# Keys of a cross-attention from quarter products: two of seven half products per whole chunk made in seven smaller ones

## The chip, the core and the metric

The kernel runs on one core of one Trainium2 chip. The metric is the time of the whole program on the device in microseconds. The engines named here are TensorE (PE, with its weight loads PEld), VectorE (DVE), ScalarE (ACT), GpSimd (POOL) and SyncE (SP), which issues the DMAs.

## The reference

One block of a perceiver: 128 latent rows attend to 12,544 context rows, then attend to themselves, then pass a mixture of experts. All is float32. What matters here is the first part, the cross-attention to the context (`cond`, 12,544 x 512), with 8 key and value groups of 128 columns and 16 query heads:

```python
def _L0_xattn_ref(...):
    ...
    kvx = jnp.einsum('bsi,oi->bso', cond, w_kv_x)
    kx, vx = jnp.split(kvx, 2, axis=-1)
    kx = _ln(kx.reshape(b, sc, g, d), kxln_w, kxln_b)
    vx = vx.reshape(b, sc, g, d)
    xout = _gqa(qx, kx, vx).reshape(b, s, nh * d)
    cat = jnp.concatenate([core, xout], axis=-1)
    catq = _div_clamp_fp8(cat, proj_smooth)
    return jnp.einsum('bsi,oi->bso', catq, wproj) * (proj_in_scale * proj_w_scale)
```

So keys and values are each the product of a 12,544 x 512 matrix with a 512 x 1024 one, the keys are normalised per group over their 128 columns, and a softmax attention runs over all 12,544 rows.

## The kernel before

**Chunks.** The context is cut into 25 chunks of 512 rows; number 12 has 256. Chunk 0 is worked in part beside the preparation of the queries. A chunk is `whole(c)` when it is not the first and has 512 rows: 23 of the 25. The loop over `c` has two stages. In the scores stage, eight groups `g` are gone through: `scores(c, g)` (PE L824) multiplies keys and queries, ACT scales them (L829), DVE takes maxima (L835); between the groups one piece each of the value products of this chunk is issued. In the key stage, eight pieces of the key products of chunk `c + 1` are issued by `keys`, and after each piece `others(g)` runs `maxima` and `outputs(c, g)` (PE L930), which weighs the values of chunk `c`.

**Products with seven in place of eight.** Weights and tokens are cut into halves in both directions, and a product of two 2 x 2 block matrices is made from seven block products (Winograd's form of Strassen's scheme). `mixed[c]` holds the seven token factors, `mixed_w` the seven weight factors; sums and differences of the tokens are made by `mix_tokens` on POOL. Two of the four quarters of the original are still used as they stand; the difference `b22 - b12` is written over `b12`, `a11 - a21` over `a21`. `unit` (L330) runs the seven products of one unit in three PSUM banks: bank `a` is copied out by ACT three times (`held`, L339) while products go on being accumulated on it, and DVE adds the other banks to the copies (L345, L353, L358). `k_unit` makes the keys so, in two units of four groups; each of the seven products is four matmuls of 256 columns (L369). `v_unit` makes the values so in chunks that are not whole.

**Values one level deeper.** For whole chunks, `v_chunk` makes two of the seven half products (numbers 1 and 3) from seven products of quarters each time, `fine(...)` (L449). The quarters' token differences come from `mix_finer_tokens` on POOL (L425 to L428), into a tile `fx` of one buffer; those of the weights come once, in chunk 0, from `mix_finer_weights` on POOL (L408 to L411).

**Banks and temporaries.** Key and value products share a pool of three PSUM banks, `ps_kv`, tag "kv": a new tile waits until an old one has been read for the last time. ACT's copies go to SBUF tiles of tag "u", three of them. In `v_chunk` the last bank `a` is read by two DVE adds (L501, L502), the last bank `d` by one (L499).

**Softmax.** `maxima(c, 4)` and `maxima(c, 8)` call `max_rows`: small DVE reductions (L852, L862) and arithmetic (L867 to L875). Then, for each pair `j` of groups, `spread` puts the shifts on all partitions (L884), DVE subtracts them (L900), and `weigh` takes exponentials on ACT (L912), and rescales and sums rows on POOL (L914, L922). Pairs 0 and 1 are handled in the scores stage, 2 and 3 in the key stage.

**Norm of the keys.** `k_sums` squares the finished keys on ACT (L511) and sums on DVE (L512), four heads at a time; `k_rstd` folds them by small matmuls on PE (L524), and POOL takes the power (L531).

**Order.** The order of the instructions on each engine is laid down when the program is built: written order gives the priority, and an instruction that is expected to be ready can go ahead of one that is not. `tc.issue_after(x)` holds the instructions in its block behind `x` on their engine. At run time each engine works through its list in that order.

Of the kernel before, what the change touches and what calls it, by code (L numbers as in the profile page):

```python
# [9 lines left out]
F32 = mybir.dt.float32  # L10
# [7 lines left out]
P = 128  # L18
# [27 lines left out]
def block_kernel(  # L46
# [56 lines left out]
    make_identity(nc, ident)  # L103
    mhalf = keep.tile([P, 16], F32, name="mhalf")
    nc.gpsimd.memset(mhalf, -0.5)
    ones = keep.tile([P, P], F32, name="ones")
    nc.gpsimd.memset(ones, 1.0)
    fold = keep.tile([P, 32], F32, name="fold")
    rcol = keep.tile([P, NCOL], F32, name="rcol")
# [219 lines left out]
    def unit(mm, view, d11, d12, d21, d22):  # L329


        a = ps_kv.tile([P, CH], F32, tag="kv", name="a_ps")
        b = ps_kv.tile([P, CH], F32, tag="kv", name="b_ps2")
        c = ps_kv.tile([P, CH], F32, tag="kv", name="c_ps")
        va, vb, vc = view(a), view(b), view(c)

        def held(name):
            t = tmpk.tile([P, CH], F32, tag="u", name=name, bufs=3)
            copied[0] = nc.scalar.copy(view(t), va).ins  # L339
            return view(t)  # L340

        mm(a, 0, True)
        p1 = held("p1")
        mm(b, 1, True)
        nc.vector.tensor_tensor(d11, vb, p1, ALU.add)  # L345
        yield
        mm(a, 5, False)
        u2 = held("u2")
        mm(c, 4, True)
        yield  # L350
        mm(a, 6, False)
        u3 = held("u3")
        nc.vector.tensor_tensor(d22, vc, u3, ALU.add)  # L353
        yield
        mm(a, 3, False)
        nc.scalar.copy(d21, va)
        mm(c, 2, False)
        added[0] = nc.vector.tensor_tensor(d12, vc, u2, ALU.add).ins  # L358
        yield
# [38 lines left out]

    finer = []

    def finer_w(i, k):

        return wkv[:, 2 + k, :, H + i * H // 2 : H + (i + 1) * H // 2]

    def mix_finer_weights(eng):
        finer.append(finp.tile([P, 4, 2, H // 2], F32, name="finer"))
        s1, s2, s3, s4 = (finer[0][:, i] for i in range(4))
        eng.tensor_tensor(s1, finer_w(1, 0), finer_w(1, 1), ALU.add)  # L408
        eng.tensor_tensor(s2, s1, finer_w(0, 0), ALU.subtract)
        eng.tensor_tensor(s3, finer_w(0, 0), finer_w(1, 0), ALU.subtract)  # L410
        eng.tensor_tensor(s4, finer_w(0, 1), s2, ALU.subtract)  # L411

    finer_x = {}

# [1 line left out]
        return c > 0 and chunks[c][1] == CH  # L416

    def mix_finer_tokens(c, eng):
        t = finp.tile([P, 2, 4, P], F32, tag="fx", name=f"finer_{c}")
        finer_x[c] = []  # L420
        for i, x in enumerate((mixed[c][1], mixed[c][3])):
            b11, b12 = x[:, 0, 0:P], x[:, 0, P : 2 * P]
            b21, b22 = x[:, 1, 0:P], x[:, 1, P : 2 * P]
            t1, t2, t3, t4 = (t[:, i, j, :] for j in range(4))
            eng.tensor_tensor(t1, b12, b11, ALU.subtract)  # L425
            eng.tensor_tensor(t2, b22, t1, ALU.subtract)
            eng.tensor_tensor(t3, b22, b12, ALU.subtract)
            eng.tensor_tensor(t4, b21, t2, ALU.subtract)  # L428
            finer_x[c].append((b11, b21, b22, t4, t1, t2, t3))

    def v_chunk(c):

        f = (
            finer_w(0, 0), finer_w(0, 1), finer[0][:, 3], finer_w(1, 1), finer[0][:, 0],
            finer[0][:, 1], finer[0][:, 2],
        )
        xs = finer_x.pop(c)

        def bank(name):
            return ps_kv.tile([P, CH], F32, tag="kv", name=name)  # L440

        def held(a, name):
            t = tmpk.tile([P, CH], F32, tag="u", name=name, bufs=3)
            copied[0] = nc.scalar.copy(t, a).ins
            return t

        def fine(ps, n, first):
            for i in range(2):
                nc.tensor.matmul(  # L449
                    ps[:, i * H // 2 : (i + 1) * H // 2], lhsT=xs[i][n], rhs=f[n][:, i, :],  # L450
                    start=first and i == 0, stop=True, skip_group_check=True,
                )

        def both(t):
            return t.rearrange("p (i o) -> p i o", i=2)

        def to(o, v):
            return V[:, v, :].rearrange("p (i c o) -> p i c o", i=2, c=2)[:, :, o, :]

        a, b = bank("fa_ps"), bank("fb_ps")  # L460
        fine(a, 0, True)
        p1 = held(a, "p1")
        fine(b, 1, True)
        nc.vector.tensor_tensor(to(0, 0), both(b), both(p1), ALU.add)
        yield
        fine(a, 5, False)
        u2 = held(a, "u2")
        d = bank("fc_ps")
        fine(d, 4, True)
        yield  # L470
        fine(a, 6, False)
        u3 = held(a, "u3")
        nc.vector.tensor_tensor(to(1, 1), both(d), both(u3), ALU.add)
        yield
        fine(a, 3, False)
        nc.scalar.copy(to(1, 0), both(a))
        fine(d, 2, False)
        nc.vector.tensor_tensor(to(0, 1), both(d), both(u2), ALU.add)
        yield
        for v in range(2):  # L480
            def mm(ps, i, first):
                w, x = mixed_w[i], mixed[c][i]
                for k in range(2):
                    last_mm[0] = nc.tensor.matmul(  # L484
                        ps, lhsT=x[:, k, v * P : (v + 1) * P], rhs=w[:, k, H : 2 * H],
                        start=first and k == 0, stop=k == 1, skip_group_check=True,
                    ).ins

            t1, t2 = V[:, v, :], V[:, 2 + v, :]
            a, d = bank("a_ps"), bank("c_ps")  # L490
            mm(a, 0, True)
            nc.vector.tensor_tensor(t1[:, :H], a, t1[:, :H], ALU.add)
            mm(d, 4, True)
            nc.scalar.copy(t2[:, H:], d)
            yield
            mm(a, 5, False)
            u2 = held(a, "u2")
            mm(d, 2, False)
            nc.vector.tensor_tensor(t2[:, :H], d, u2, ALU.add)  # L499
            mm(a, 6, False)  # L500
            nc.vector.tensor_tensor(t2[:, H:], a, t2[:, H:], ALU.add)  # L501
            added[0] = nc.vector.tensor_tensor(t1[:, H:], a, t1[:, H:], ALU.add).ins  # L502
            yield
# [38 lines left out]
    def keys(c, others, pool, tag, todo=None, done=0):  # L542

        sums = {}
        todo = todo or parts(k_unit(c, u) for u in range(2))
        for i in range(done, 8):
            next(todo)
            if i % 4 == 3:
                sums[i // 4] = k_sums(c, i // 4)
            if others:  # L550
                others(i)
            if i == (6 if others else 4):
                with ExitStack() as first:
                    if not others:
                        first.enter_context(tc.high_priority())
                        first.enter_context(tc.issue_after(cores[2]))
                    k_rstd(c, 0, sums.pop(0), pool, tag)
        return sums

    with tc.tile_pool(name="pre", bufs=2) as pre, tc.tile_pool(name="pre1", bufs=1) as pre1, tc.tile_pool(  # L560
# [115 lines left out]
            begin(names[0])  # L676
        with tc.issue_after(begun[0][1]):
            nc.tensor.transpose(psb[:, :P], gains[:, 3:4].to_broadcast([P, P]), ident)
            nc.tensor.matmul(psb[:, P:], lhsT=ones, rhs=gains[:, 5:6], start=True, stop=True)
            nc.scalar.copy(kb, psb)  # L680
        for k in range(NK):
            wk_in = wkvT[k * P : (k + 1) * P, : G * D].rearrange("p (u h o) -> p u h o", u=2, h=2)
# [117 lines left out]


    finp = main.enter_context(tc.tile_pool(name="finp", bufs=1))
    olp = late.enter_context(tc.tile_pool(name="olp", bufs=1, side="right", reuse_waits="tile"))
    ol = [olp.tile([P, 2, HS], F32, name=f"ol{g}") for g in range(G)]
    rlat = keep.tile([S, NH], F32, name="rlat")
# [168 lines left out]
    def maxima(c, i):  # L974

        if i in (4, 8):
            max_rows(c, i // 2 - 2, 2)
        j = i // 4 * 2 - 2 + (i - 1) % 4
        if i in (5, 6, 9, 10):

            last = copied[0]
            if c == 0 and i == 6:
                weigh(c, 0, last)
            if c == NCH // 2 and i == 10:
                weigh(c, 2, last)
            spread(c, j)
            if (c, j) in ((0, 0), (NCH // 2, 2)):
                return
            wait = (c, j) in ((0, 3), (NCH // 2 - 1, 2)) or whole(c) and j == 0
            weigh(c, j, last if wait else None)  # L990

    for c in range(NCH):
# [7 lines left out]
        for g in range(G):  # L1000
# [10 lines left out]
            if g == 2 and c + 1 < NCH:  # L1011
                with tc.issue_after(summed[0] if c else made):
                    for step in mix_tokens(c + 1):
                        step()
                    if c == 0:
                        mix_finer_weights(nc.gpsimd)
            if g == 4 and c + 1 < NCH and whole(c + 1):
                mix_finer_tokens(c + 1, nc.gpsimd)

# [1 line left out]
        def others(g):  # L1021
            maxima(c, G + g)
            outputs(c, g)

        if c + 1 < NCH:
            sums = keys(c + 1, others, ps_t, "t")
# [386 lines left out]
```

## Time and profile before

| | |
|---|---|
| median of 3 runs | 2154.01 us (2148.28, 2154.01, 2210.41) |
| profiled execution | 2148.35 us, of which the span from first to last instruction 2146.6 us |
| granted TensorE clock | 1.000 |
| busy: PE, DVE, ACT, POOL | 2121.8, 1366.1, 918.5, 1174.8 us |
| before the chunk loop | 126.7 us |
| chunks 0, 11 and 12 | 61.8, 65.5 and 53.2 us |
| each other chunk up to 23 | 75.8 us: scores stage 37.4, key stage 38.4 |
| from the scores of chunk 24 on | 247.8 us |

The chunk that the prediction reads closely is number 5: its scores stage begins at 491.69 us from the span's start, its key stage (keys of chunk 6) at 529.10, and the next chunk's scores at 567.47. In a row of the profile, "x8" counts instructions, and an fp32 matmul as written in the kernel is two of them. The ends of matmuls are modelled and overlap, so distances are taken from start to start.

### The profile page before, as it was taken

How to read it: one execution, taken by the hardware profiler on the slowest of the kernel's cores; microseconds unless marked ns; L12 is line 12 of the kernel's file. 1: busy time of each engine (PE TensorE's matmuls, PEld its weight loads, DVE VectorE, ACT ScalarE, POOL GpSimd, SP SyncE). 2: the span in 40 equal slices, each digit the busy share in tenths (PEclk: the TensorE clock that was granted, in tenths of full speed). 3: DMA queues.
4: the chain of work that ended last, by engine and by line, in shares of the span. 5: the costliest groups of instructions: out<-in, count | busy, mean ns of one | idle time of the engine just before them, and what ended most of it. 6: DMA issues, size and time to landing. Idle time of an engine off the chain costs nothing.

```text
span 2146.6 us, 24680 instructions
## 1 busy us (share of the span) xinstructions
PE 2121.8 (99%) x8935; PEld 1580.9 (74%) x8935; DVE 1366.1 (64%) x2452; ACT 918.5 (43%) x1787; POOL 1174.8 (55%) x1359
## 2 busy tenths in 40 slices
PE   8999999999999999999999999999999999999999
PEld 3667877877877787787777877887787787777554
DVE  8776576577567657656676567557657756767311
ACT  3445355445435434444444445445544543551211
POOL 5345675575576567447575576567557557633000
PEclk9999999999999999999999999999999999999999
DMA  9300000000000000000000000000000000007793
GB/s 320 117 20 1 20 20 0 20 20 20 1 20 20 1 21 20 10 1 20 20 20 3 19 20 20 1 20 20 1 20 20 20 1 20 1 1 264 218 286 110
DMA packets 71226, 95.54 MB, mean 45 GB/s; under 512 B 3136, under 2 KB 39488, under 8 KB 71104
## 3 DMA queue, kind: packets, MB, share of 16 engines
q1 hardware_dynamic: 70816, 93.92, 13.2%
q8 instruction: 70, 1.15, 0.2%
q14 instruction: 52, 0.43, 0.1%
q10 hardware_dynamic: 288, 0.04, 0.0%
HBM read 93.69 MB, written 0.26 MB: 44 GB/s over the span
## 4 chain that ended last, share of the span: by engine, by line
PE 93%; DVE 3%; issue 2%; DMA 1%; ACT 1%; POOL 0%; SPq 0%; POOLq 0%; DVEq 0%; ACTq 0%
PE s_ps L824 15%; PE a_ps L369 15%; PE o_ps L930 15%; PE a_ps L484 11%; PE c_ps L369 8%; PE c_ps L484 7%; PE gu_ps L1328 4%; PE fa_ps L449 4%; PE b_ps L369 4%; PE moe_acc L1349 2%; PE fc_ps L449 2%; PE ps_p L625 1%; PE fb_ps L449 1%; PE a_ps L388 1%; PE ps_core L785 1%
## 5 line engine op out<-in xcount | busy, mean ns | idle before, releaser
L922 POOL TENSOR_TENSOR ol<-ol,s 128x256 f32<-128x256 f32 x764 | 550.7, 729 | 40.3 <-POOL ol L914 0.4
L531 POOL TENSOR_TENSOR krs<-kve,mhalf 128x16 f32<-128x16 f32 (+1 forms) x50 | 142.7, 2855 | 434.3 <-DVE kve L529 434.3
L824 PE MATMUL s_ps<-qxT,KT 128*128 128x256 f32 x1568 | 372.8, 381 | 0.4 <-ACT s L829 0.4
L930 PE MATMUL o_ps<-s,V 128*128 128x256 f32 x1568 | 370.7, 379 | 0.9 <-DVE ol L935 0.9
L914 POOL TENSOR_TENSOR ol<-ol,al 128x512 f32<-128x512 f32 x192 | 242.8, 1276 | 213.6 <-DVE al L884 213.6
L829 ACT ACTIVATE s<-s_ps,krs 128x256 f32<-128x256 f32 x784 | 321.4, 470 | 86.1 <-PE s_ps L824 51.9
L824 PEld LDWEIGHTS s_ps<-qxT,KT 128*128 128x128 f32 x1568 | 295.8, 190 | 72.8 <-issue 35.6
L835 DVE TRANSPOSE_TENSOR_REDUCE mxr<-s 128x32 f32<-128x1024 f32 (+1 forms) x200 | 244.2, 1221 | 137.9 <-ACT s L829 136.7
L930 PEld LDWEIGHTS o_ps<-s,V 128*128 128x128 f32 x1568 | 297.1, 190 | 41.6 <-ACT s L912 1.3
L912 ACT ACTIVATE s<-s 128x1024 f32<-128x1024 f32 (+1 forms) x200 | 205.9, 1041 | 183.3 <-DVE s L900 181.2
L900 DVE TENSOR_TENSOR s<-s,b_ps 128x1024 f32<-128x1024 f32 (+1 forms) x200 | 231.4, 1177 | 0.0
L512 DVE TRANSPOSE_TENSOR_REDUCE sqr<-sq 128x16 f32<-128x512 f32 (+1 forms) x200 | 138.9, 694 | 87.5 <-ACT sq L511 87.3
L511 ACT ACTIVATE sq<-KT 128x512 f32<-128x512 f32 (+1 forms) x200 | 124.8, 624 | 158.9 <-DVE KT L358 90.8
L369 PE MATMUL a_ps<-ctx,wkv 128*128 128x256 f32 (+1 forms) x800 | 185.6, 375 | 0.0
L484 PE MATMUL a_ps<-wkv,ctx 128*128 128x512 f32 x368 | 172.9, 592 | 0.0
L369 PEld LDWEIGHTS a_ps<-ctx,wkv 128*128 128x128 f32 x800 | 150.0, 190 | 29.4 <-issue 10.5
L935 DVE TENSOR_TENSOR ol<-ol,o_ps 128x256 f32<-128x256 f32 x192 | 78.4, 409 | 135.1 <-PE o_ps L930 134.0
L339 ACT COPY u<-a_ps 128x512 f32<-128x512 f32 (+1 forms) x106 | 60.8, 574 | 202.2 <-PE a_ps L369 197.2
L358 DVE TENSOR_TENSOR KT<-c_ps,u 128x512 f32<-128x512 f32 (+1 forms) x50 | 34.0, 681 | 143.6 <-PE c_ps L369 143.6
L484 PEld LDWEIGHTS a_ps<-wkv,ctx 128*128 128x128 f32 x368 | 69.9, 190 | 68.4 <-issue 66.0
L369 PE MATMUL a_ps<-mix,wkv 128*128 128x256 f32 (+1 forms) x400 | 95.9, 382 | 2.6 <-POOL ol L922 2.6
L876 ACT ACTIVATE als<-als 128x32 f32<-128x32 f32 x48 | 11.0, 229 | 200.7 <-DVE als L875 200.7
(282 smaller groups left out, 3129.0 us busy)
## 6 DMA issues: line engine op xcount, KB each, us to landing
ctx<-in_ctxT SPq DMA_DIRECT2D x23, 1024.0 KB, 5.1
gu<-in_w SPq DMA_DIRECT2D x32, 384.0 KB, 4.9
gu<-in_v SPq DMA_DIRECT2D x32, 384.0 KB, 5.6
dn<-in_w SPq DMA_DIRECT2D x16, 768.0 KB, 5.7
w<-in_wprojT SPq DMA_DIRECT2D x8, 1024.0 KB, 5.8
w<-in_wqxT SPq DMA_DIRECT2D x4, 1024.0 KB, 11.0
w<-in_wqT SPq DMA_DIRECT2D x4, 1024.0 KB, 7.1
wkv<-in_wkvT SPq DMA_DIRECT2D x8, 256.0 KB, 8.3
```

What stands on the lines that cost most here:

```text
L369: nc.tensor.matmul(ps[:, j * h : (j + 1) * h], lhsT=w[:, k, (2 * u + j) * D : (2 * u + j + 1) * D], rhs=x[:, k, :], start=first and j == k ...
L449: nc.tensor.matmul(ps[:, i * H // 2 : (i + 1) * H // 2], lhsT=xs[i][n], rhs=f[n][:, i, :], start=first and i == 0, stop=True, skip_group_c ...
L484: last_mm[0] = nc.tensor.matmul(ps, lhsT=x[:, k, v * P : (v + 1) * P], rhs=w[:, k, H : 2 * H], start=first and k == 0, stop=k == 1, skip_g ...
L531: nc.gpsimd.tensor_tensor(rs[:, :, :nt], ve[:, :, :nt], mhalf.rearrange("p (g t) -> p g t", g=4)[:, :, :nt], ALU.pow,)
L824: end = nc.tensor.matmul(ps[:, t - t0, :], lhsT=KT[:, g, t * P : (t + 1) * P], rhs=qxT[:, 2 * g : 2 * g + 2, :], start=True, stop=True,)
L829: copied[0] = nc.scalar.activation(s[:, t, :], ps[:, t - t0, :], AF.Copy, scale=rs[:, t : t + 1]).ins
L835: nc.vector.tensor_reduce(mxr[g // 4][:, g % 4, :nt, :].rearrange("p t k -> p (t k)"), s[:, :nt, :].rearrange("p t (k i) -> p (t k) i", i=32),
L900: nc.vector.tensor_tensor(s[:, :nt, :], s[:, :nt, :], ps[:, a, None, :].to_broadcast([P, nt, HS]), ALU.subtract,)
L912: nc.scalar.activation(s[:, :nt, :], s[:, :nt, :], AF.Exp, scale=scale)
L914: nc.gpsimd.tensor_tensor(ol[g], ol[g], rescale[j][:, a, None, :].to_broadcast([P, 2, HS]), ALU.mult)
L922: summed[0] = nc.gpsimd.tensor_tensor(ol[g][:, 1, :], first, s[:, t, :], ALU.add).ins
L930: end = nc.tensor.matmul(ps, lhsT=V[:, t, g * D : (g + 1) * D], rhs=s[:, t, :], start=t == 0, stop=t == nt - 1,)
```

## The change

For whole chunks `keys` now runs `k_chunk` in place of two `k_unit`s. It does for the keys what `v_chunk` does for the values: half products 1 and 3 of both units are made at once from seven products of quarters, each four matmuls of 128 columns, in banks `fb`, `fa` and `fc`; then the five remaining half products of each unit follow in banks `a_ps` and `c_ps`, and DVE adds them onto the keys that the quarters left in `KT`. The quarter differences of tokens and weights that stood in tiles of their own (`t3`, `s3`) are written over the quarters that they replace. Since chunk 12 needs the weights as they were, `turn_finer_weights` undoes and redoes this around it. The mix of the key weights is made in chunk 0 on DVE, that of the value weights in the key stage of chunk 0 on POOL. `k_sums` of the first unit follows piece 4 in place of piece 3, and `k_rstd` comes ahead of `others(6)`. The exponentials of pairs 2 and 3 are held behind the latest ACT copy, as those of pair 0 were. Tiles of tag "u" go from three to two, and a tile of ones from 128 columns to one.

```diff
-    ones = keep.tile([P, P], F32, name="ones")
+    ones = keep.tile([P, 1], F32, name="ones")
...
-            t = tmpk.tile([P, CH], F32, tag="u", name=name, bufs=3)
+            t = tmpk.tile([P, CH], F32, tag="u", name=name)
...
+    def mix_finer_weights(v, eng):
+        s1, s2, s4 = (finer[0][:, v, i] for i in range(3))
+        eng.tensor_tensor(s1, finer_w(v, 1, 0), finer_w(v, 1, 1), ALU.add)
+        eng.tensor_tensor(s2, s1, finer_w(v, 0, 0), ALU.subtract)
+        turn_finer_weights(v, eng)
+        eng.tensor_tensor(s4, finer_w(v, 0, 1), s2, ALU.subtract)
+
+    def turn_finer_weights(v, eng):
+        eng.tensor_tensor(finer_w(v, 1, 0), finer_w(v, 0, 0), finer_w(v, 1, 0), ALU.subtract)
...
-            eng.tensor_tensor(t3, b22, b12, ALU.subtract)
+            eng.tensor_tensor(b12, b22, b12, ALU.subtract)
             eng.tensor_tensor(t4, b21, t2, ALU.subtract)
-            finer_x[c].append((b11, b21, b22, t4, t1, t2, t3))
+            finer_x[c].append((b11, b21, b22, t4, t1, t2, b12))
...
+    def k_chunk(c):
+        f, xs, h = finer_factors(0), finer_x[c], CH // 2
+
+        def fine(ps, n, first):
+            for j in range(4):
+                i, g = j // 2, j % 2
+                nc.tensor.matmul(
+                    ps[:, j * P : (j + 1) * P], lhsT=f[n][:, i, g * D : (g + 1) * D],
+                    rhs=xs[i][n], start=first and j == 0, stop=True, skip_group_check=True,
+                )
...
+        b, a, d = bank("fb_ps"), bank("fa_ps"), bank("fc_ps")
+        fine(b, 1, True)
+        fine(a, 0, True)
+        p1 = kept(a, "p1", groups)
+        add(to(0, 0), groups(b), p1)
+        fine(d, 4, True)
+        fine(a, 5, False)
+        u2 = kept(a, "u2", groups)
+        a0 = bank("a_ps")
+        mm(a0, 0, 0, True)
+        yield
+        fine(a, 6, False)
+        u3 = kept(a, "u3", groups)
+        add(to(1, 1), groups(d), u3)
+        yield
+        fine(a, 3, False)
+        copied[0] = nc.scalar.copy(to(1, 0), groups(a)).ins
+        fine(d, 2, False)
+        add(to(0, 1), groups(d), u2)
+        add(out(0, 0, 0), pair(a0), out(0, 0, 0))
+        yield
+        d0 = bank("c_ps")
+        mm(d0, 0, 4, True)
+        nc.scalar.copy(out(0, 1, 1), pair(d0))
+        mm(a0, 0, 5, False)
+        u2 = kept(a0, "u2", pair)
+        yield
+        mm(d0, 0, 2, False)
+        add(out(0, 0, 1), pair(d0), u2)
+        mm(a0, 0, 6, False)
+        add(out(0, 1, 1), pair(a0), out(0, 1, 1))
+        add(out(0, 1, 0), pair(a0), out(0, 1, 0))
+        a1 = bank("a_ps")
+        mm(a1, 1, 0, True)
+        add(out(1, 0, 0), pair(a1), out(1, 0, 0))
+        yield
...
     def keys(c, others, pool, tag, todo=None, done=0):
-        todo = todo or parts(k_unit(c, u) for u in range(2))
+        fine = whole(c)
+        todo = todo or (k_chunk(c) if fine else parts(k_unit(c, u) for u in range(2)))
         for i in range(done, 8):
             next(todo)
-            if i % 4 == 3:
-                sums[i // 4] = k_sums(c, i // 4)
+            if i in ((4, 7) if fine else (3, 7)):
+                sums[i // 7] = k_sums(c, i // 7)
+            if fine and i == 6:
+                k_rstd(c, 0, sums.pop(0), pool, tag)
             if others:
                 others(i)
...
-            wait = (c, j) in ((0, 3), (NCH // 2 - 1, 2)) or whole(c) and j == 0
+            wait = (c, j) in ((0, 3), (NCH // 2 - 1, 2)) or whole(c) and j != 1
             weigh(c, j, last if wait else None)
...
+                if c == 0:
+                    mix_finer_weights(0, nc.vector)
+            if c == NCH // 2 - 1 and g == 5 or c == NCH // 2 and g == 2:
+                turn_finer_weights(0, nc.gpsimd)
...
         def others(g):
             maxima(c, G + g)
             outputs(c, g)
+            if g == 3:
+                if c == 0:
+                    mix_finer_weights(1, nc.gpsimd)
+                elif c in (NCH // 2 - 1, NCH // 2):
+                    turn_finer_weights(1, nc.gpsimd)
```

The second unit's pieces, left out here, repeat those of the first with banks `a1` and `d1`.

More of the change, by code (lines that the diff above doesn't have):

```diff
@@ L399, in block_kernel, with finer_w @@
     finer = []
[L401 to L411, printed above, removed]
+    def finer_w(v, i, k):
+        x = v * H + i * H // 2
+        return wkv[:, 2 + k, :, x : x + H // 2]
+    def mix_finer_weights(v, eng):
[6 more added lines that the diff above has]
+        eng.tensor_tensor(finer_w(v, 1, 0), finer_w(v, 0, 0), finer_w(v, 1, 0), ALU.subtract)
     finer_x = {}
@@ L418, in mix_finer_tokens @@
     def mix_finer_tokens(c, eng):
-        t = finp.tile([P, 2, 4, P], F32, tag="fx", name=f"finer_{c}")
+        t = finp.tile([P, 2, 3, P], F32, tag="fx", name=f"finer_{c}")
         finer_x[c] = []
@@ L423, in mix_finer_tokens @@
             b21, b22 = x[:, 1, 0:P], x[:, 1, P : 2 * P]
-            t1, t2, t3, t4 = (t[:, i, j, :] for j in range(4))
+            t1, t2, t4 = (t[:, i, j, :] for j in range(3))
             eng.tensor_tensor(t1, b12, b11, ALU.subtract)
             eng.tensor_tensor(t2, b22, t1, ALU.subtract)
-            eng.tensor_tensor(t3, b22, b12, ALU.subtract)
+            eng.tensor_tensor(b12, b22, b12, ALU.subtract)
             eng.tensor_tensor(t4, b21, t2, ALU.subtract)
-            finer_x[c].append((b11, b21, b22, t4, t1, t2, t3))
@@ L431, in v_chunk @@
-    def v_chunk(c):
[L433 to L445, printed above, removed]
+            finer_x[c].append((b11, b21, b22, t4, t1, t2, b12))
@@ new lines, in finer_factors, with bank, kept, mm @@
+    def finer_factors(v):
+        s1, s2, s4 = (finer[0][:, v, i] for i in range(3))
+        w = [[finer_w(v, i, k) for k in range(2)] for i in range(2)]
+        return w[0][0], w[0][1], s4, w[1][1], s1, s2, w[1][0]
+    def bank(name):
+        return ps_kv.tile([P, CH], F32, tag="kv", name=name)
+    def kept(a, name, view=lambda t: t):
+        t = tmpk.tile([P, CH], F32, tag="u", name=name)
+        copied[0] = nc.scalar.copy(t, a).ins
+        return view(t)
+    def k_chunk(c):
[7 more added lines that the diff above has]
+                )
+        def mm(ps, u, i, first):
+            w, x = mixed_w[i], mixed[c][i]
+            for j in range(2):
+                for k in range(2):
+                    nc.tensor.matmul(
+                        ps[:, j * h : (j + 1) * h],
+                        lhsT=w[:, k, (2 * u + j) * D : (2 * u + j + 1) * D], rhs=x[:, k, :],
+                        start=first and j == k == 0, stop=j == k == 1, skip_group_check=True,
+                    )
+        def groups(t):
+            return t.rearrange("p (g t) -> p g t", g=4)
+        def pair(t):
+            return t.rearrange("p (g t) -> p g t", g=2)
+        def to(u, v):
+            return KT[:, 4 * u : 4 * u + 4, v * P : (v + 1) * P]
+        def out(u, i, j):
+            return KT[:, 4 * u + 2 * i : 4 * u + 2 * i + 2, j * h : (j + 1) * h]
+        def add(o, a, b):
+            return nc.vector.tensor_tensor(o, a, b, ALU.add).ins
+        b, a, d = bank("fb_ps"), bank("fa_ps"), bank("fc_ps")
[34 more added lines that the diff above has]
+        yield
+        d1 = bank("c_ps")
+        mm(d1, 1, 4, True)
+        nc.scalar.copy(out(1, 1, 1), pair(d1))
+        mm(a1, 1, 5, False)
+        u2 = kept(a1, "u2", pair)
+        yield
+        mm(d1, 1, 2, False)
+        add(out(1, 0, 1), pair(d1), u2)
+        yield
+        mm(a1, 1, 6, False)
+        add(out(1, 1, 1), pair(a1), out(1, 1, 1))
+        added[0] = add(out(1, 1, 0), pair(a1), out(1, 1, 0))
+        yield
@@ L447, in fine @@
+    def v_chunk(c):
+        f, xs = finer_factors(1), finer_x.pop(c)
         def fine(ps, n, first):
@@ L461, in v_chunk @@
         fine(a, 0, True)
-        p1 = held(a, "p1")
+        p1 = kept(a, "p1")
         fine(b, 1, True)
@@ L466, in v_chunk @@
         fine(a, 5, False)
-        u2 = held(a, "u2")
+        u2 = kept(a, "u2")
         d = bank("fc_ps")
@@ L471, in v_chunk @@
         fine(a, 6, False)
-        u3 = held(a, "u3")
+        u3 = kept(a, "u3")
         nc.vector.tensor_tensor(to(1, 1), both(d), both(u3), ALU.add)
@@ L496, in v_chunk @@
             mm(a, 5, False)
-            u2 = held(a, "u2")
+            u2 = kept(a, "u2")
             mm(d, 2, False)
@@ L544, in keys @@
         sums = {}
-        todo = todo or parts(k_unit(c, u) for u in range(2))
+        fine = whole(c)
+        todo = todo or (k_chunk(c) if fine else parts(k_unit(c, u) for u in range(2)))
         for i in range(done, 8):
             next(todo)
-            if i % 4 == 3:
-                sums[i // 4] = k_sums(c, i // 4)
+            if i in ((4, 7) if fine else (3, 7)):
+                sums[i // 7] = k_sums(c, i // 7)
+            if fine and i == 6:
+                k_rstd(c, 0, sums.pop(0), pool, tag)
             if others:
                 others(i)
+            if fine:
+                continue
             if i == (6 if others else 4):
@@ L678, in block_kernel @@
             nc.tensor.transpose(psb[:, :P], gains[:, 3:4].to_broadcast([P, P]), ident)
-            nc.tensor.matmul(psb[:, P:], lhsT=ones, rhs=gains[:, 5:6], start=True, stop=True)
+            nc.tensor.matmul(
+                psb[:, P:], lhsT=gains[:, 5:6].to_broadcast([P, P]), rhs=ones, start=True, stop=True
+            )
             nc.scalar.copy(kb, psb)
@@ L802, in block_kernel @@
     finp = main.enter_context(tc.tile_pool(name="finp", bufs=1))
+    finer.append(finp.tile([P, 2, 3, 2, H // 2], F32, name="finer"))
     olp = late.enter_context(tc.tile_pool(name="olp", bufs=1, side="right", reuse_waits="tile"))
@@ L1014, in block_kernel @@
                         step()
-                    if c == 0:
-                        mix_finer_weights(nc.gpsimd)
+                if c == 0:
+                    mix_finer_weights(0, nc.vector)
+            if c == NCH // 2 - 1 and g == 5 or c == NCH // 2 and g == 2:
+                turn_finer_weights(0, nc.gpsimd)
             if g == 4 and c + 1 < NCH and whole(c + 1):
```

## The prediction

> **What bounds the kernel now.** First the page's engine line and its chain of waits, then the busy times by stretch.
>
> ```profile
> PE 2121.8 (99%) x8935; PEld 1580.9 (74%) x8935; DVE 1366.1 (64%) x2452; ACT 918.5 (43%) x1787; POOL 1174.8 (55%) x1359
> ...
> PE 93%; DVE 3%; issue 2%; DMA 1%; ACT 1%; POOL 0%; SPq 0%; POOLq 0%; DVEq 0%; ACTq 0%
> ```
> ```profile
> 491.69:529.10 37.41, 37.41 (x142) 25.15 (x140) 30.52 (x50) 23.00 (x48) 21.59 (x28) 1.00 0.00 1
> 529.10:567.47 38.37, 38.37 (x185) 33.51 (x184) 19.39 (x35) 11.96 (x18) 25.28 (x27) 1.00 0.08 28
> 529.10:541.00 11.90, 11.90 (x57) 10.48 (x56) 11.03 (x19) 5.33 (x7) 8.36 (x11) 1.00 0.26 89
> ```
> The columns of the second view are stretch and length, then busy microseconds of PE, PEld, DVE, ACT and POOL with their instruction counts, then granted clock and DMA. One chunk in the steady part is 75.8 us: 37.4 us of scores with the value products between them, 38.4 us of key products with the outputs between them. TensorE has not a microsecond of idle time, at clock 1.00. So PE work taken out is time gained, and any wait put before a PE instruction is time lost in full. The third row is the one to keep: in the first 12 us of the key stage DVE is busy 11.03 of 11.90 us. Over the whole stage it has half its time free, at its start it has none.
>
> **PE work.** A written fp32 product shows as two matmul instructions. In the key stage of the short chunk 12 they are 128 columns wide, in whole chunks 256:
>
> ```profile
> 1008.30 1.16 PE L369 MATMUL a_ps<-mix,wkv 128*128 128x128 f32 x8
> 1009.29 1.06 PE L369 MATMUL c_ps<-ctx,wsum 128*128 128x128 f32 x8
> 1010.19 1.03 PE L930 MATMUL o_ps<-s,V 128*128 128x256 f32 x4
> ```
> ```profile
> 527.38 1.88 PE L484 MATMUL a_ps<-wkv,ctx 128*128 128x512 f32 x4
> 529.10 1.89 PE L369 MATMUL a_ps<-ctx,wkv 128*128 128x256 f32 x8
> 530.83 1.89 PE L369 MATMUL b_ps<-ctx,wkv 128*128 128x256 f32 x8
> 532.55 1.89 PE L930 MATMUL o_ps<-s,V 128*128 128x256 f32 x8
> ```
> Go by start to start, since the ends overlap. Eight narrow instructions, each with its own weights, take 1010.19 - 1009.29 = 0.90 us, 0.112 each; eight wide ones 530.83 - 529.10 = 1.73 us, 0.216 each. Removed per whole chunk: half products 1 and 3, in two units, four matmuls each, so 16 written and 32 instructions, 32 x 0.216 = 6.91 us. Added: seven quarter products of four narrow matmuls, 28 written and 56 instructions, 56 x 0.112 = 6.27 us. Gain 0.64 us a chunk; 23 whole chunks (1 to 11, 13 to 24) make 14.7 us, 0.7% of the run. No more than this can be won.
>
> A rule of the Trainium skill speaks against narrow products. "TensorE: Matmul & The Clock Gate", section "Back-to-back issue gap", puts a stream of weight loads and 128-column matmuls at about 81 ns each where the bare gap is 56, because the load no longer hides. Scaled by 81/56, the narrow instruction here would be an estimated 0.16 us, the added work 9.1 us, and the change would lose 2.2 us a chunk before any wait, 50 us in all. The row above has a weight load for each matmul and still 0.112 us, so I leave the rule out of the sum.
>
> **The work off PE.** ACT has eight copies a chunk before and after (four in each of two units; p1, u2, u3, u2, u2 and three straight into KT). DVE goes from six key adds to eleven: five more by 0.69 us (L358's mean, 691 ns) is 3.4 us a chunk, 19.4 to 22.8 in the 38 us of the stage: hidden, except where DVE is full. POOL's eight token operations at 0.45 us are the same, half in place. They end at 507.8, and are now wanted at about 531 rather than after 567: 23 us of cover (13 us in chunk 0, from 134.0 to 146.95). The weights' mix for the keys is four DVE operations once (L244's 702 ns for such a shape: 2.8 us), beside waits of 3.56, 0.48 and 1.67 us that DVE has between 126 and 136; that for the values is four POOL operations of 1.27 us (5 us), moved to a stage where POOL is free from 176.5 to 183.75 and not wanted before 190. The four turns of weights, 1.27 us of POOL each, fall beside chunks 11 and 12, where POOL is busy 76 of 119 us. Each of these costs its own length once if the cover is missing, 5 us at most. The single column of ones serves one product before the main loop: nothing.
>
> Two temporaries "u" rather than three: the slot of a new copy was last read two copies back. The tightest is the new u3 (about 539), after the first add's p1 (read by 535.0); a miss would be 0.6 us.
>
> The exponentials of pairs 2 and 3 (ACT L912) are held behind the key copies u3 and the copy to quarter (1,0). They now start at 534.5 and 538.9 and would start 3 to 5 us later. Behind them on ACT are only key copies. Who waits: the outputs of heads 4 to 7, the first of them 12 us after, and POOL's row sums. POOL ends its chunk at 555.5 and then idles 7.2 us before the next power (krs L531): 5 of 7.2. Nothing.
>
> k_sums moves from piece 3 to piece 4, k_rstd to before output 6. The latter's matmuls stood 5.5 us ahead of the next scores (562.00 against 567.47), and will stand 1.73 + 1.73 + 1.73 + 0.2 = 5.4 ahead. Its operands (squares and reductions, 1.41 us a head) are complete about 3 us sooner than that. Nothing.
>
> **What gets onto the path: the third bank.** ps_kv has three banks. The second half of the value products holds two of them when the key stage starts, and DVE empties them:
>
> ```profile
> 529.00 0.69 DVE L499 TENSOR_TENSOR V<-c_ps,u 128x512 f32<-128x512 f32 x1
> ...
> 531.44 0.67 DVE L501 TENSOR_TENSOR V<-a_ps,V 128x512 f32<-128x512 f32 x1
> 532.03 0.67 DVE L502 TENSOR_TENSOR V<-a_ps,V 128x512 f32<-128x512 f32 x1
> 532.62 0.69 DVE L884 STREAM_TRANSPOSE al<-als 128x512 f32<-128x512 f32 x1
> 533.23 1.18 DVE L900 TENSOR_TENSOR s<-s,b_ps 128x1024 f32<-128x1024 f32 x1
> 534.34 0.68 DVE L345 TENSOR_TENSOR KT<-b_ps,p 128x512 f32<-128x512 f32 x1
> ```
> Before, the stage's third bank (c_ps) is first written at 536.0, long after L502 let it go at 532.70. In the changed code the stage opens with fine(b), fine(a), fine(d): the first takes the free bank, the second the one that L499 frees at 529.69 (wanted at 530.0: just in time), the third is wanted at 529.10 + 2 x 0.896 = 530.89 and has to wait for L502: **1.81 us of idle PE**. Queued behind it on PE are a5, a0 and output 0, all later by it.
>
> Next late: the product a0 needs a fourth bank, that of b, which the first key add (L345's successor) frees. After the wait PE reaches a0 at 532.7 + 2 x 0.896 = 534.5. If that add goes ahead of the first L900 it ends at 533.9, no wait; if behind, as now, at 535.0: 0.5 us. The order within an engine is laid down when the program is built, from what is expected to be ready. The short chunk, whose add is ready 1.6 us sooner, has it ahead:
>
> ```profile
> 986.75 0.67 DVE L502 TENSOR_TENSOR V<-a_ps,V 128x512 f32<-128x512 f32 x1
> 987.34 0.69 DVE L884 STREAM_TRANSPOSE al<-als 128x512 f32<-128x512 f32 x1
> 987.95 0.39 DVE L345 TENSOR_TENSOR KT<-b_ps,p 128x256 f32<-128x256 f32 x1
> 988.26 1.21 DVE L900 TENSOR_TENSOR s<-s,b_ps 128x1024 f32<-128x1024 f32 x1
> ```
> It also shows that another width of the key products moves L501 and L502 not at all: they end 3.6 us after its key stage starts at 983.82, as in whole chunks. The new add is ready about 1 us sooner than the old, between the two cases: I take half, 0.25 us.
>
> The order can also soften the wait: PE is not held to the written order either. In chunk 0 a value product is cut in two by scores written before it:
>
> ```profile
> 125.89 1.02 PE L388 MATMUL c_ps<-wsum,mix 128*128 128x512 f32 x2
> 126.74 3.62 PE L824 MATMUL s_ps<-qxT,KT 128*128 128x256 f32 x16
> 130.20 1.02 PE L388 MATMUL c_ps<-wsum,mix 128*128 128x512 f32 x2
> ```
> If one matmul of output 0 (0.43 us) is drawn ahead of fine(d), 1.4 us is left; if the whole output (1.73 us), 0.1. Bounds for the bank are so 0.1 and 1.81 us, and for a0 0 and 0.5; I take 1.65 + 0.25 = 1.9 us a chunk, nearest to the rows as they stand. The later banks are freed with 2 us or more to spare, as DVE has caught up by about 541.
>
> **Sum.** 1.9 - 0.64 = +1.26 us for the 21 whole chunks that follow a whole one (2 to 11, 14 to 24): 26.5 us. Chunks 1 and 13 follow stages with waits of 2.7 and 1.0 us already, and with all value banks free; I put gain and new waits there at 0, between -4 and +4. The profiled run took 2148.35 us for a span of 2146.6, and 1.75 outside it is kept: 2148.35 + 26.5 = **2175 us**. That run is the fastest of those shown; their median, 2154.01, lies 0.3% higher. A measurement of this kernel tells about 2%, 43 us, from no change, so this is "same", on the slow side.
>
> **Rivals.** *The bank never waits* (0.21): output 0 goes ahead, or L501 and L502 come before the row maxima. For: PE's order is free; against: L501 and L502 kept their place in the short chunk. 2148.35 - 14.7 = 2134 us, faster than before; any total wait under 0.64 us a chunk puts it on this side.
>
> *DVE's backlog takes the next bank too* (0.14): the first key add queues behind both L900 of pair 2 and ends at 532.62 + 0.61 + 2 x 1.1 + 0.68 = 536.1, so that a0 waits 1.6 us more. For: DVE is full until 540. Against: the add is ready sooner than now, and now it stands between the two. 1.81 + 1.6 - 0.64 = 2.77, by 21 = 58: 2206 us. It passes 2% from 2.7 us of waits a chunk.
>
> *Narrow products don't pay* (0.02): if an instruction cost the 190 ns that its weight load shows in the page, 56 x 0.19 = 10.6 us against 6.9, 23 x 3.7 = 85 us: 2233. The spacing of 0.112 us speaks against it.
>
> **Numbers.** The forecast has 0.63, and alone spans 2160 to 2188 (waits of 1.4 to 2.3 us and the two odd chunks). The range takes in the first rival, whose 2134 is the floor, and goes up half of the way to the second: 2133 to 2196; what is left out is most of the last two rivals. Faster by over 2% has no mechanism, as PE gives 0.7%: 0.01. Slower by over 2%: the last two rivals and a tail of the forecast, 0.17. Within: 0.82.
>
> **What would show it.** Right: 368 fewer wide and 644 more narrow written key products, at 0.112 us; in the list of waits PE fc_ps (lhsT K) ended by DVE L502's successor some 21 times, 1.4 to 1.9 us each; a key stage of about 39.6 us, scores still 37.4; DVE at about 1444 us. Wrong: PE idle still 0.00 in a steady chunk with output 0 ahead of fine(d); DVE's V adds ahead of the row maxima; or waits on ACT or POOL, which I put at nothing.

## The result and the profile after

The changed kernel takes 2174.05 us (median of 4 runs, 2170.52 to 2174.74), the kernel before 2153.97 (median of 4, 2148.28 to 2210.41). The execution of 2210.41 us, 2.9% above the fastest, was a slow one and is left out of the ratio. The ratio is 1.010 [1.0086, 1.0114]: slower by 1%, inside the 2% that the prediction calls "same". The profiled execution after took 2170.52 us, its span is 2168.4 us against 2146.6.

The engine line and the summary of the chain of waits on the page of the kernel after:

```profile
PE 2114.5 (98%) x9487; PEld 1582.4 (73%) x9487; DVE 1441.3 (66%) x2571; ACT 919.8 (42%) x1787; POOL 1185.6 (55%) x1363
PE 84%; DVE 9%; issue 3%; ACT 2%; POOL 1%; DMA 1%; SPq 0%; POOLq 0%; ACTq 0%; DVEq 0%
```

TensorE has less to do (2121.8 us before) and still the span is longer: DVE's share of the chain that ends last has gone from 3% to 9%. Where it comes in, the busy times by stretch of the kernel after show (chunk 5: scores stage, key stage, first 11.9 us of the key stage; the columns are those of the same view before):

```profile
494.73:532.16 37.43, 37.43 (x142) 25.16 (x141) 29.34 (x48) 22.37 (x47) 21.60 (x28) 1.00 0.00 0
532.16:571.50 39.34, 37.99 (x209) 33.52 (x208) 23.75 (x41) 12.64 (x20) 25.48 (x27) 1.00 0.08 28
532.16:544.06 11.90, 10.55 (x71) 9.49 (x70) 11.70 (x20) 3.56 (x6) 6.58 (x7) 1.00 0.26 89
```

The scores stage is as long as before. The key stage is 0.97 us longer, and the idle time of PE in it, 39.34 - 37.99 = 1.35 us, lies in its first 12 us, where DVE is busy 11.70 of 11.90. The list of waits after has the wait by name, with total, count and mean:

```profile
PE fc_ps L455 <- DVE V L594: 28.7, 21, 1.4
```

PE's timeline after, at the start of that key stage (start, length, engine, line, operation; idle time before it and its releaser in brackets):

```profile
533.94 0.60 PE L1031 MATMUL o_ps<-s,V 128*128 128x256 f32 x2
535.89 1.13 PE L455 MATMUL fc_ps<-finer,finer 128*128 128x128 f32 x8 [1.35 <-DVE V L594]
536.86 1.06 PE L455 MATMUL fa_ps<-finer,finer 128*128 128x128 f32 x8
537.75 0.60 PE L1031 MATMUL o_ps<-s,V 128*128 128x256 f32 x2
538.18 1.92 PE L464 MATMUL a_ps<-ctx,wkv 128*128 128x256 f32 x8
```

DVE's timeline after, same place:

```profile
532.76 0.37 DVE L963 TENSOR_REDUCE m_new<-mx 32x32 f32<-32x128 f32 x1
...
533.85 0.73 DVE L985 STREAM_TRANSPOSE b_ps<-sh 128x512 f32<-128x512 f32 x1
534.48 0.67 DVE L593 TENSOR_TENSOR V<-a_ps,V 128x512 f32<-128x512 f32 x1
535.07 0.67 DVE L594 TENSOR_TENSOR V<-a_ps,V 128x512 f32<-128x512 f32 x1
535.67 0.68 DVE L985 STREAM_TRANSPOSE al<-als 128x512 f32<-128x512 f32 x1
536.28 1.18 DVE L1001 TENSOR_TENSOR s<-s,b_ps 128x1024 f32<-128x1024 f32 x1
537.38 0.68 DVE L483 TENSOR_TENSOR KT<-fb_ps,p 128x512 f32<-128x512 f32 x1
537.98 1.21 DVE L1001 TENSOR_TENSOR s<-s,b_ps 128x1024 f32<-128x1024 f32 x1
```

The third quarter product wants a bank at 533.94. DVE lets the bank go only at 535.74, after the last value add (L594), because a row-maximum reduction, the arithmetic on the maxima and a transpose (532.76 to 534.48) stand before the two adds. In PE's list one written matmul of output 0 (0.43 us) stands ahead of that product, and then PE stands still. The rest of this document counts in chunk lengths: from the first score matmul of a chunk to that of the next in the trace, median over the steady whole chunks. They are 75.787 us before and 76.776 after, +0.99.

### The profile page after: what moved, and what is told of

Read it like the earlier page. It is cut to its first block, busy times and chain, and to the rows that moved or that the text cites. A ratio compares the mean times of both kernels' runs of the same rounds, so it can differ in the third digit from the quotient of the medians.

```text
span 2168.4 us, 25820 instructions
## 1 busy us (share of the span) xinstructions
PE 2114.5 (98%) x9487; PEld 1582.4 (73%) x9487; DVE 1441.3 (66%) x2571; ACT 919.8 (42%) x1787; POOL 1185.6 (55%) x1363
## 4 chain that ended last, share of the span: by engine, by line
PE 84%; DVE 9%; issue 3%; ACT 2%; POOL 1%; DMA 1%; SPq 0%; POOLq 0%; ACTq 0%; DVEq 0%
PE s_ps L925 15%; PE o_ps L1031 14%; PE a_ps L464 11%; PE a_ps L576 8%; PE c_ps L464 7%; PE c_ps L576 6%; PE gu_ps L1436 4%; PE fa_ps L541 4%; PE fa_ps L455 3%; PE fc_ps L455 2%; PE moe_acc L1457 2%; PE fc_ps L541 2%; DVE mx L953 2%; PE ps_p L722 1%; DVE mxr L936 1%
## 5 line engine op out<-in xcount | busy, mean ns | idle before, releaser
L1031 PE MATMUL o_ps<-s,V 128*128 128x256 f32 x1568 | 380.6, 381 | 0.9 <-DVE ol L1036 0.9
L1031 PEld LDWEIGHTS o_ps<-s,V 128*128 128x128 f32 x1568 | 288.1, 190 | 36.4 <-ACT s L1013 1.3
L1013 ACT ACTIVATE s<-s 128x1024 f32<-128x1024 f32 (+1 forms) x200 | 201.3, 1040 | 80.3 <-DVE s L1001 80.2
L1001 DVE TENSOR_TENSOR s<-s,b_ps 128x1024 f32<-128x1024 f32 (+1 forms) x200 | 232.8, 1175 | 0.0
L464 PE MATMUL a_ps<-ctx,wkv 128*128 128x256 f32 x736 | 170.8, 380 | 0.0
L464 PEld LDWEIGHTS a_ps<-ctx,wkv 128*128 128x128 f32 x736 | 138.0, 190 | 21.4 <-DVE KT L483 3.5
L445 ACT COPY u<-fa_ps 128x512 f32<-128x512 f32 x92 | 54.0, 587 | 145.2 <-PE fa_ps L455 144.2
L483 DVE TENSOR_TENSOR KT<-a_ps,KT 128x512 f32<-128x512 f32 x138 | 89.2, 673 | 6.3 <-PE a_ps L464 5.6
L1436 PE MATMUL gu_ps<-gu,xT 128*128 128x384 f32 x256 | 87.4, 486 | 0.0
```

Of the source, the lines that this page charges most:

```text
L464: nc.tensor.matmul(ps[:, j * h : (j + 1) * h], lhsT=w[:, k, (2 * u + j) * D : (2 * u + j + 1) * D], rhs=x[:, k, :], start=first and j == k ...
L1001: nc.vector.tensor_tensor(s[:, :nt, :], s[:, :nt, :], ps[:, a, None, :].to_broadcast([P, nt, HS]), ALU.subtract,)
L1013: nc.scalar.activation(s[:, :nt, :], s[:, :nt, :], AF.Exp, scale=scale)
L1031: end = nc.tensor.matmul(ps, lhsT=V[:, t, g * D : (g + 1) * D], rhs=s[:, t, :], start=t == 0, stop=t == nt - 1,)
L1436: nc.tensor.matmul(ps, lhsT=xT[:, k, :], rhs=experts[x][0][i][:, k], start=k == 0, stop=k == NK - 1,)
```

## Experiments

Two things had to be told apart: whether the wait for the bank is the whole loss (then, without it, PE's gain of 0.64 us a chunk appears), and whether anything else in the change costs time. The kernel before was run beside all of them: 2153.04 us in the first set, 2152.51 in the second. The first set was e1 to e4, the second e5 to e8.

**e1_pin: the fourth reduction held behind the value adds.** The change, with one of the four small reductions of the row maxima, and with it all that follows from the maxima, put behind L594 on DVE. Nothing else is held by hand.

```diff
-        with tc.issue_after(added[0]) if c == NCH - 1 and j0 else nullcontext():
-            for b in range(4):
+        for b in range(4):
+            held = c == NCH - 1 or b == 3 and whole(c)
+            with tc.issue_after(added[0]) if held and j0 else nullcontext():
```

> The changed kernel with one order altered on DVE: in whole chunks the fourth of the row-maximum reductions (and with it the rest of the maxima's chain) is held behind the last value adds, so that the adds that free the third bank run some 1.3 us sooner. Theory (the third bank is what costs; narrow products gain 0.64 us a chunk; all else is hidden): the wait of fc_ps for the last value add falls from 1.35 to 0.1 us or less, a whole chunk from 76.77 to about 75.2 us, the kernel from 2172 to 2136 to 2140 us, below the kernel before. Rival 1 (narrow products gain nothing, the weight load of each shows): the wait goes as well, but a chunk ends at 75.8 us or more, the kernel at 2148 to 2155. Rival 2 (DVE's five further adds are what costs): the wait moves to another bank and the kernel stays above 2160.

Measured: 2147.57 us, ratio 0.9972 [0.9963, 0.9982]; chunk 75.484, that is 1.29 less than after and 0.30 less than before. DVE's timeline of e1_pin, in which the key stage begins at 527.08:

```profile
528.19 0.68 DVE L594 TENSOR_TENSOR V<-a_ps,V 128x512 f32<-128x512 f32 x1
528.90 0.36 DVE L964 TENSOR_REDUCE m_new<-mx 32x32 f32<-32x128 f32 x1
...
530.61 0.67 DVE L483 TENSOR_TENSOR KT<-fb_ps,p 128x512 f32<-128x512 f32 x1
```

PE's timeline of e1_pin:

```profile
528.42 0.61 PE L455 MATMUL fa_ps<-mix,wkv 128*128 128x128 f32 x4
529.02 1.13 PE L455 MATMUL fc_ps<-finer,finer 128*128 128x128 f32 x8
529.98 1.06 PE L455 MATMUL fa_ps<-finer,finer 128*128 128x128 f32 x8
530.88 0.60 PE L1032 MATMUL o_ps<-s,V 128*128 128x256 f32 x2
531.34 1.99 PE L464 MATMUL a_ps<-ctx,wkv 128*128 128x256 f32 x8
533.16 1.46 PE L1032 MATMUL o_ps<-s,V 128*128 128x256 f32 x6
```

L594 now ends at 528.87, 1.79 us after the stage began instead of 3.58. `fc_ps` starts at 529.02, 0.15 us after that end and 0.15 after the 528.87 at which PE is free for it. Two orders followed the hold by themselves: the first key add (L483) now stands ahead of the subtractions (L1002), and no matmul of output 0 stands ahead of `fc_ps`. The trace says which of this counts. From start to start, 0.15 us is lost ahead of `fc_ps` in place of 1.52 (533.94 + 0.43 to 535.89), which is 1.37 less, and the small delays behind it are about 0.1 larger: 1.27 of the 1.29. So the queue position of the two adds was the loss.

Neither rival's condition is met (a chunk of 75.8 us or more; a kernel above 2160). But the size fell short of what was expected: of the ideal -0.64 a chunk only -0.30 came. In the trace, start to start, 0.15 us of the rest is the late `fc_ps`, 0.07 is lost within it (0.96 to the next product, where eight narrow instructions take 0.90), 0.03 in the two instructions of output 0 ahead of the first half product a0, and 0.09 within a0, whose bank the first key add frees at 531.28 (1.82, where eight wide ones take 1.73): these are the missing 0.34. The time of 2136 to 2140 us was missed with it: 0.28 us over 21 chunks is 6 of the 8 to 12 us.

**e2_order: output 0 between the second and the third quarter product.** The written order gives PE other work while DVE gets to the adds; the later pieces, `k_sums` and `k_rstd` move along.

```diff
         add(to(0, 0), groups(b), p1)
+        yield
         fine(d, 4, True)
...
         add(out(1, 0, 1), pair(d1), u2)
-        yield
         mm(a1, 1, 6, False)
```

> The changed kernel with the order altered on PE instead: output 0 stands between the second quarter product and the third, so that PE has 1.73 us of other work while the third bank is being freed; the key pieces after it move by one, and the last two are one piece. Theory: the third product comes at 3.5 us after the start of the stage, where its bank is free at 3.6, so 0.1 to 0.2 us of waiting is left; chunk about 75.3 us, kernel 2136 to 2142 us. Rival 1: chunk 75.8 us or more, kernel 2148 to 2155. Rival 2: above 2160.

Measured: 2156.57 us, 1.0014 [1.0006, 1.0023]; chunk 75.914, 0.86 less than after, but 0.13 more than before. The expectation was missed. PE's timeline of e2_order (the key stage begins at 528.55):

```profile
530.34 1.89 PE L1031 MATMUL o_ps<-s,V 128*128 128x256 f32 x8
532.30 1.13 PE L455 MATMUL fc_ps<-finer,finer 128*128 128x128 f32 x8
533.27 1.06 PE L455 MATMUL fa_ps<-finer,finer 128*128 128x128 f32 x8
534.53 1.99 PE L464 MATMUL a_ps<-ctx,wkv 128*128 128x256 f32 x8 [0.20 <-DVE KT L483]
536.36 1.89 PE L1031 MATMUL o_ps<-s,V 128*128 128x256 f32 x8
```

DVE's timeline of e2_order:

```profile
531.49 0.67 DVE L594 TENSOR_TENSOR V<-a_ps,V 128x512 f32<-128x512 f32 x1
...
532.69 1.18 DVE L1001 TENSOR_TENSOR s<-s,b_ps 128x1024 f32<-128x1024 f32 x1
533.79 0.68 DVE L483 TENSOR_TENSOR KT<-fb_ps,p 128x512 f32<-128x512 f32 x1
```

Two waits remain. The adds end at 532.16 and the output at 530.34 + 1.73 = 532.07, so `fc_ps` is still 0.23 late. And a0, which now has no matmul of output 0 to stand in front of it, waits for the first key add (L483): that stands behind the first L1001 and ends at 534.47, 0.30 after the 534.17 at which a0 is wanted, and a0 starts at 534.53, 0.36 late. This is the second wait of the prediction, which the kernel after does not have. PE work moved into one gap was taken from the next. The chunk lies where rival 1 had put it (75.8 us or more), but not for rival 1's reason: the two starts, 0.23 and 0.36 late, and 0.07 and 0.10 within the products that waited make 0.76 of the 0.77 that is missing from -0.64.

**e3_narrow: the price of narrow matmuls alone.** The kernel before, its products 1 and 3 written as twice as many matmuls of 128 columns, with the same sums and banks.

```diff
+        n = h // 2 if i in (1, 3) and whole(c) else h
...
+                    for y in range(0, h, n):
-                        ps[:, j * h : (j + 1) * h],
+                            ps[:, j * h + y : j * h + y + n],
```

> The kernel before, in whole chunks half products 1 and 3 of the keys issued as twice as many matmuls of 128 columns, each with its own weight load; the arithmetic is the same. Theory: 64 instructions of 0.112 us in place of 32 of 0.216, 7.17 against 6.91 us, so 0.26 us more a chunk, 23 x 0.26 = 6 us: 2154 us beside 2148. Rival 1 (the weight load shows, an estimate of 0.16 us an instruction): 3.5 us more a chunk, 2228 us.

Measured: 2158.36 us, 1.0028 [1.0017, 1.0038]; chunk 76.027, +0.24 for 32 more instructions with the same columns in all, where 0.26 was expected; the kernel is 5.3 us above the kernel before beside it, where 6 was expected. PE's timeline of e3_narrow:

```profile
531.82 1.95 PE L371 MATMUL b_ps<-ctx,wkv 128*128 128x128 f32 x16
533.60 1.89 PE L933 MATMUL o_ps<-s,V 128*128 128x256 f32 x8
```

Sixteen narrow instructions take 533.60 - 531.82 = 1.78 us, 0.111 each, where eight wide ones of the same work took 1.73. The rule of the Trainium skill ("TensorE: Matmul & The Clock Gate", section "Back-to-back issue gap") that the prediction weighed does not hold for the fp32 matmuls of this run: by its 81 ns against 56, scaled, the same edit would have been an estimated 2228 us. No other type was run here.

**e4_rest: all of the change but the quarter products.** The keys' loop keeps the old units; the weights' mixes and turns, the differences in place, two temporaries, the held exponentials and the single column of ones stay.

```diff
-        fine = whole(c)
+        fine = False
```

> The changed kernel with the keys of whole chunks made by the two old units of seven half products and the old places of the sums: all other parts of the change stay (two temporaries, differences in place, held exponentials, weights mixed on DVE, turned weights). The turned weights and tokens enter the old products here, so the keys of whole chunks are other numbers. Theory: none of these parts costs anything: chunk 75.8 us with no idle PE, kernel 2146 to 2151 us. Rival 3 (the held exponentials, the two temporaries or the work in place cost part of it): a chunk above 75.9 us, 2152 to 2165 us.

Measured: 2153.24 us, 1.0001 [0.9993, 1.001]; chunk 75.787, to the third decimal that of before. All these parts together cost nothing. The run stands for times alone, as its keys of whole chunks are other numbers, and it leaves out the five further key adds and the moves of `k_sums` and `k_rstd`.

**e5_nopin: exponentials of pairs 2 and 3 set free again.** e1_pin with the old rule for them.

```diff
-            wait = (c, j) in ((0, 3), (NCH // 2 - 1, 2)) or whole(c) and j != 1
+            wait = (c, j) in ((0, 3), (NCH // 2 - 1, 2)) or whole(c) and j == 0
```

> The version with one reduction held, without the part of the change that holds the exponentials of pairs 2 and 3 behind the key copies on ACT. Theory of the prediction (that part costs nothing and nothing on the path asks for it): chunk 75.5 us as with it. Rival 4 (ACT works its list in order, an exponential that waits for DVE's subtraction then stands ahead of the key copies u2 and u3, and the next quarter product waits for them): 0.4 to 1.5 us more a chunk, 9 to 32 us.

Measured: 2145.88 us, 0.9971 [0.9959, 0.9983]; chunk 75.481 against 75.484. Holding them neither costs nor saves.

**e6_late: is it DVE's load?** e1_pin with two of the later key adds made three times each, four more DVE adds a chunk, all after DVE has caught up.

```diff
-        add(out(0, 0, 1), pair(d0), u2)
+        for _ in range(3):
+            add(out(0, 0, 1), pair(d0), u2)
```

> The version with one reduction held, and two of the later key adds of each chunk (those of bank c_ps with u2, one in each unit) made three times over, with the same operands and result: four more DVE adds of 0.69 us a chunk, 2.8 us, in the part of the key stage where DVE has time. Theory (only the first 12 us of the stage are full): chunk 75.48 us, no change. Rival 2 (DVE's count of adds is what the change costs): up to 2.8 us more a chunk, at least 0.5 us; 21 x 0.5 = 10 us or more.

Measured: 2147.63 us, 0.9974 [0.9965, 0.9983]; chunk 75.482. The engine line on its page:

```profile
PE 2114.4 (99%) x9487; PEld 1584.9 (74%) x9487; DVE 1499.3 (70%) x2663; ACT 917.2 (43%) x1787; POOL 1184.6 (55%) x1363
```

DVE is busy 60 us longer than in e1_pin (1439.0 us), and the chunk is the same, 75.482 against 75.484. It is also busy 58 us longer than after, with a chunk 1.29 us shorter. So the count of DVE's adds is not the cost; the place of the adds that free a bank in its queue is. The run says this of adds late in the stage; more adds at its full start were not tried.

**e7_pin_before: would the hold help the kernel before as well?** The kernel before with the edit of e1_pin.

> The kernel before with the same reduction held behind the last value adds. There the third bank is first written 3.3 us after it is free. Theory: no idle PE to win, chunk 75.79 us as before, ratio 1.000. Rival 5 (the order on DVE is better for other reasons, whatever the key products): a chunk under 75.7 us, ratio 0.998 or less.

Measured: 2154.03 us, 1.0005 [0.9996, 1.0014]; chunk 75.787. It does nothing there: no PE work was waiting for those adds. What e1_pin wins belongs to the quarter products.

**e8_pin2: two of four reductions held.** `b >= 2 and whole(c)` in place of `b == 3 and whole(c)`.

> As the version with one row-maximum reduction held behind the last value adds, but with two of the four held, so that those adds run 0.37 us sooner still. There the third quarter product still starts 0.15 us late (0.262 against 0.112 us from start to start), and the kernel is 0.28% faster than before. Theory: that 0.15 us goes, a whole chunk from 75.48 to 75.33 us, 21 x 0.15 = 3 us, ratio to before about 0.996. Rival (the late start is a cost of the narrow products themselves, not of the bank): chunk stays at 75.48 us, ratio 0.997.

Measured: 2146.34 us, 0.9966 [0.9954, 0.9978]; chunk 75.367, 0.42 less than before and 1.41 less than after. PE's timeline of e8_pin2:

```profile
527.95 0.61 PE L455 MATMUL fa_ps<-mix,wkv 128*128 128x128 f32 x4
528.39 1.06 PE L455 MATMUL fc_ps<-finer,finer 128*128 128x128 f32 x8
529.38 1.13 PE L455 MATMUL fa_ps<-finer,finer 128*128 128x128 f32 x8
530.35 1.97 PE L464 MATMUL a_ps<-ctx,wkv 128*128 128x256 f32 x8
```

`fc_ps` follows 0.44 us after the four narrow instructions ahead of it, their own time: no wait is left there, and the rival (a late start that belongs to narrow products) falls. The chunk came down by 0.12 of the expected 0.15 us, as the next hand-overs now show: the product behind `fc_ps` starts 0.09 us late, 0.14 after ACT has copied its bank out (529.24), and loses 0.07 more until a0 starts at 530.35. By its chunk this is the best version that was run, a third of a percent faster than the kernel before and 1.3% faster than the changed kernel; the median of e5_nopin, 2145.88, differs from it by less than the runs of either spread.

## Why the prediction was right

**The narrow products pay: right.** 0.112 us was the price in the prediction; e3_narrow has 0.111. The rival of 0.19 us an instruction falls with it. The gain itself is read from e8_pin2: 0.42 us a chunk came, and 0.09 + 0.07 us of delays are seen at the product behind `fc_ps` and 0.07 in a0 (530.35 to 532.15, 1.80 where 1.73 would do). Together that is 0.65 beside the 0.64.

**The edits at nothing: right.** e4_rest and e5_nopin show it for ACT, POOL, the mixes and the holds, e6_late for additional adds late in the stage. The moves of `k_sums` and `k_rstd` were not tried alone, but the sum of e8_pin2 leaves nothing for them. DVE's 1441.3 us stand against 1444.

**The third bank: right in mechanism, place and count, a little too large.** The wait is in the list 21 times, as said, ended by L594, which is L502's successor. The term was 1.65 us; measured in chunk 5, from the 534.37 at which PE is free (533.94 + 0.43) to 535.89, it is 1.52 (the list has 1.35, as it counts from the matmul's modelled end). The prediction named the case: one written matmul of output 0 drawn ahead leaves 1.4. That is what happened, and 0.15 us were added by the start 0.15 after the add's end, which the prediction's 1.81 did not have.

**The bank of a0: the order was left open, the cost was put too high.** The prediction took half of 0.5 us. The first key add does stand behind the first L1001 (537.38 to 538.06), the worse of its two cases. But a0 lost nothing, since one more matmul of output 0 fills 537.75 to 538.18. e2_order takes that matmul away and has the wait.

**The sum.** 0.99 us a chunk against 1.26: 1.52 - 0.64 = 0.88, and some 0.1 of small delays within the third product and a0. Over 21 chunks that is 20.8 us of the 21.8 by which the span grew. The others: chunk 0's period -0.8, chunk 11's -0.5, chunk 12's +1.0, the part from chunk 24 on +1.5, before the loop -0.1. The prediction had +26.5 and 0 for the rest. That its 2175 us lies 1 us beside the median of 2174 is luck: the growth was put 5.7 us too high (26.5 against 20.8), and the base, 2148.35, the fastest run of before, lies 5.6 us under that kernel's median of 2153.97. The range, 2133 to 2196, held the first rival too; it is the list of waits, not the time, that tells the two apart.

**The rivals.** The bank that never waits (2134) did not happen by itself: output 0 went ahead by one matmul and not by all. e1_pin and e8_pin2 make this case by hand, and the times, 2147.57 and 2146.34, show that its price was too good: of the 14.7 us that it took off the fastest run of before, 6 and 7.3 came beside the kernel before (ratios 0.9972 and 0.9966), since 0.07 to 0.15 us of delay stay at the hand-overs of banks. DVE's backlog reaching the next bank (2206) had the order wrong: the first key add stands behind one subtraction (L1001, 536.28), not behind both (537.98), and PE had a matmul of output 0 to fill the time. The prediction had the value adds ahead of the row maxima only as an order that the build might choose. It did not weigh that one line can lay it down and turn the result: the hold on the reductions, which the kernel had for the last chunk already.

## What to carry to other kernels

With PE full, this change was decided by which bank its first products need and by what the releasing engine has queued ahead of the release; look at the first microseconds of the stage, not at the engine's mean. Move the releasing instruction ahead in its own queue before the matmuls are reordered around it: filling one gap with matmuls emptied the next (e2_order). A queue position costs nothing until somebody waits for it, so an order that suited the old kernel (e7_pin_before) says nothing about the new one.

## What the runs showed of the hardware

**The hand-over of a bank.** In chunk 5 the first matmul into a bank starts 0.14 to 0.15 us after the end of the DVE add that frees it (after 535.74 to 535.89, e1_pin 528.87 to 529.02, e2_order 532.16 to 532.30). A product that had to wait then loses another 0.07 to 0.10 us within itself (`fc_ps` 0.96 or 0.97 in place of 0.90 in these three runs; a0 of e2_order 1.83 in place of 1.73).

**The granted clock.** The chunk lengths of kernels that differ only off the path agree to 0.01 us (75.787 in before, e4_rest and e7_pin_before; 75.481 to 75.484 in e1_pin, e5_nopin and e6_late), but the part from the scores of chunk 24 on came in steps: 247.7 to 247.8 us (before, e6_late, e8_pin2), 249.3 (after), 251.8 (e1_pin, e5_nopin, e7_pin_before) and 253.5 (e2_order, e3_narrow, e4_rest). In the runs of the last three steps the granted clock of PE falls to half for a while in this part. Busy times by stretch of e1_pin (the granted clock is the third number from the end):

```profile
1988.60:1998.84 10.24, 9.82 (x39) 8.08 (x39) 1.69 (x5) 2.18 (x5) 0.00 (x0) 0.50 0.35 116
```

The dip lasts 10.2 us in e1_pin, 3.4 in the kernel after (from 2020.2, also at 0.50), and the slowest three have one of each; against the first step they cost 4, 1.5 and 5.7 us. This is why e1_pin and e6_late have spans of 2144.2 and 2139.9 us with the same chunk. It would also explain the spread of the kernel before, 2148 to 2154: its runs at 2148.1 and 2148.4 us have a mean granted clock of 1.000, those at 2154 us 0.996 or 0.997. e8_pin2 has one dip of 3.4 us elsewhere, from 1012.9, in chunk 12, which takes 57.2 us there and 55.3 in e6_late. The Trainium skill, "TensorE: Matmul & The Clock Gate", section "What's actually happening", describes a gate to half clock after an idle window of about 3.4 us that runs free of the program; the trace agrees in the 0.5 and in lengths of one and three times 3.4 us, but not in the idle window. In the 3.4 us ahead of the dip of e1_pin PE is busy 2.47 us with no gap over 0.7, and ahead of the first dip of e4_rest, at 1962.9, it is busy for all 3.41, mostly with matmuls of one column. What the gate counts, and which run gets which dip, was not tried.
